# The order of work in a recurrence period, and 704 channels split as 4 x 128 + 2 x 96

## The chip, the cores and the metric

The kernel runs on one core of one Trainium2 chip. The metric is the device time of one execution in microseconds (us). TensorE (PE) multiplies matrices, VectorE (DVE), ScalarE (ACT) and GpSimd (POOL) work on elements, and SyncE (SP) issues transfers between memory and the core's buffers. Everything is computed in float32.

## The reference

Two layers over x of shape 16 x 512 x 256 (16 sequences, 512 time steps, 256 channels), each sublayer followed by a layer norm of its sum with its input:

```
x = layernorm(x + attention(x))             # 16 heads, latents of 32, rotary, causal softmax
x = layernorm(x + fp4_mlp(x))               # 256 -> 704 (gate, up) -> 256
x = layernorm(x + recurrence(x))            # 16 heads, state of 64, 512 steps
x = layernorm(x + channel_mix(x))           # r * (relu(k)^2 @ Wv)

fp4_mlp:      h = silu(q(x) @ q(Wg).T) * (q(x) @ q(Wu).T);  q(h) @ q(Wd).T
              # q: 4-bit grid with one scale for each block of 16 channels, kept as float32
recurrence:   xn = x * rsqrt(mean(x^2) + eps) * norm_w
              state = tanh(state @ tanh(a) + xn_t @ b)           # one after the other in t
              out   = x + (state @ c + skip * xn) @ Wout + bout
channel_mix:  xr, xk = mix of x_t and x_(t-1);  sigmoid(xr @ Wr) * (relu(xk @ Wk)^2 @ Wv)
```

## The kernel before

The kernel has two stages.

**The first stage** goes over the 16 sequences. Its loop is over slots of attention scores (four groups of heads and three slots of rows each). Between the pieces of a slot it takes steps from a list written by hand (PLAN, line 635) that hold the other work: head projections, latents, values, output projection, and the feed-forward tiles of the two sequences before. A feed-forward tile has 128 tokens. `ffn_up` makes its 704 channels, `fp4` quantizes them on DVE and POOL, and `ffn_down` (line 312) turns them into the layout that the down product needs: six transposes on PE into two PSUM banks, evacuated by ACT (lines 323, 325, 326) into the tile hT. Then six matmuls (line 158) accumulate over the channels into ps_d, each with one part of hT as weights and one part of wdT, the down weights, as the moving operand. A float32 matmul of this kind appears in the trace as two instructions. The 704 channels are cut as five parts of 128 and one of 64, so hT and wdT are filled to 128 rows in five parts, and to 64 in the sixth. The three feed-forward tiles of the last sequence that remain are done in the second stage, where DVE evacuates and each product is cut in two halves of 64 output rows.

**The second stage** is the recurrence over 512 time steps, for all 16 sequences at once. The heads form two groups, g = 0 and 1. A step of one group is a recurrence block on PE (`advance_state`, line 1054: 4 matmuls, 8 in the trace) that adds state times ta to what lies in a PSUM bank u, and a tanh on ACT (line 1062) that writes the new state into hist. The inputs of a step, xn times b, are put into u ahead of time (`inputs`, line 1016). While ACT computes the tanh of one group, PE works on the other group and on pieces of other work. PE's order is fixed by the program; the other engines' order is found by a scheduler that simulates the program.

This other work is cut into periods of 16 steps. In period M, `beside(M)` gives the list of its pieces, each a call of a generator up to its next `yield`:

- N, `normed`: the first piece loads 256 tokens (SP), squares and sums them on DVE (line 855), and scales them on POOL (lines 859 to 863); the second transposes them on PE (ps_xn) and DVE writes the result to xt (line 868).
- R, `read_out`: matmuls of the clean states with wc into one bank (line 1032), and the addition of the skip on DVE into ot (line 1039).
- A, `out_of_recurrence`: four products with woutT (ps_a, line 900), then the residual, the statistics and the norm on DVE and POOL (x3, lines 917, 82 to 90, 887).
- M, `mixes`: four transposes of x3 (ps_x), the copy x3T (line 930), the difference d (line 934), and the two mixes muk and mur (line 938), on DVE.
- K, `key`: four products (ps_k); relu on DVE (ka, line 954) and the square on POOL.
- G, `gate`: four products (ps_rr); tanh on ACT (th, line 971).
- V, `value`: four products (ps_kv); on DVE th times ps_kv, the sum x, statistics, norm (o, lines 986 to 992); SP writes o out.

All of these share two PSUM banks of the pool ps_2. A piece that opens a new tile there waits until what was in its bank has been read. A fixed weight is yielded with each piece, and `some` hands out pieces so that a share of the period's total weight is spent in each step: 0.3 of it between the two groups' blocks, 0.7 after both. The pace comes from the table TIME (line 1097). The list of a period before is, from `beside` (line 1069):

```
for name, i in (
    ("N", M + 2), *[("K", old)] * 4, *[("G", old)] * 2, ("R", p), *[("G", old)] * 2,
    *[("A", p)] * 4, *[("V", old)] * 3, ("M", p), ("N", M + 2), ("V", old),
):
```

with p = M - 1 and old = M - 2. History copies (lines 1185 to 1193) on POOL and DVE move the states of eight steps at a time from hist to the clean tiles that the read-out takes.

Of the kernel before, what the change touches and what calls it, by code (L numbers as in the profile page):

```python
# [19 lines left out]
P = 128  # L20
# [3 lines left out]
FF = 704  # L24
NFB = 6
LN_EPS = 1e-5
RMS_EPS = 1e-4
# [30 lines left out]
def tile_kernel(ctx: ExitStack, tc: tile.TileContext, I: dict, out: bass.AP):  # L58
# [156 lines left out]
    def ffn_weights():  # L215
# [20 lines left out]
        for r in range(2):  # L236
            w = ffn.tile([P, FF], F32, tag="h", name="w", bufs=2)
            nc.sync.dma_start(w, I["w_down"][r * P : r * P + P, :])
            wq4 = ffn.tile([P, FF], F32, tag="hq", name="wq4", bufs=2)
            for _ in fp4(wq4, w, FF // 16):  # L240
                pass
            yield 0.3
            for k0 in (0, 3):
                ps = mm("ps_t")
                for kb in range(k0, k0 + 3):
                    n = min(P, FF - kb * P)
                    at = (kb - k0) * P
                    nc.tensor.transpose(ps[:n, at : at + P], wq4[:, kb * P : kb * P + n], ident)
                    nc.scalar.copy(wdT[:n, kb, r * P : r * P + P], ps[:n, at : at + P])
                yield 1.5  # L250
# [61 lines left out]
    def ffn_down(b, j):  # L312
        vector_done(("h", b, j))
        hq, x = hq_of.pop((b, j)), x_of[b][:, j, :]
        hT = ffn.tile([P, NFB, P], F32, tag="hT", name="hT")
        for k0, k1 in ((0, 4), (4, NFB)):
            ps = mm("ps_h")
            for kb in range(k0, k1):
                n = min(P, FF - kb * P)
                at = (kb - k0) * P  # L320
                nc.tensor.transpose(ps[:n, at : at + P], hq[:, kb * P : kb * P + n], ident)
            if k0 == 0:
                copier[0](hT[:, 0:4, :].rearrange("p k t -> p (k t)"), ps)  # L323
            else:
                copier[0](hT[:, 4, :], ps[:, :P])
                copier[0](hT[:64, 5, :], ps[:64, P : 2 * P])
        yield 0.7, True
        ps = mm("ps_d")
        for kb in range(NFB):
            n = min(P, FF - kb * P)  # L330
            product_of[0](ps[:, :C], hT[:n, kb, :], wdT[:n, kb, :], kb == 0, kb == NFB - 1)
            if kb < NFB - 1:
                yield 0.43, False
        nc.vector.tensor_tensor(x, ps[:, :C], x, ALU.add)
        layernorm(x, x)
        at_row = xs.rearrange("(t b) c -> b t c", b=B)
        nc.sync.dma_start(at_row[b, j * P : j * P + P, :], x)
        if j == NT - 1:
            x_of.pop(b)
        yield 0.45, True  # L340
# [507 lines left out]
    def normed(p):  # L848
# [17 lines left out]
        for cc in range(2):  # L866
            for t, at, n in in_ring(cc, p * TS):
# [3 lines left out]
                )  # L871
        yield 0.45

# [28 lines left out]
    def out_of_recurrence(p):  # L902
# [6 lines left out]
        for i in range(2):  # L909
            own = slice(i * C, i * C + C)  # L910
            for cc in range(2):
                product(ps[:, own], ot[:, cc, i * P : i * P + P], sq["woutT"][:, cc, :], cc == 0)
                if cc == 0:
                    yield 0.43
            if i == 0:
                yield 0.43
        nc.vector.scalar_tensor_tensor(
# [5 lines left out]
        normalized(x3, x3, mv)  # L923
        yield 0.43

    def mixes(p):
# [8 lines left out]
        for mu in ("muk", "mur"):  # L935
            mx = mix_of[p, mu] = wk2.tile([P, 2, 2 * P], F32, tag=mu, name=mu)
            for cc in range(2):
                nc.vector.scalar_tensor_tensor(
                    mx[:, cc, :], d[:, cc, :], col(mu, cc), xT[:, cc, : 2 * P], ALU.mult, ALU.add
                )  # L940
        yield 0.45

    def key(p):
        ps, mx = mm("ps_k"), mix_of.pop((p, "muk"))
        ka = ka_of[p] = wk2.tile([P, 2, 2 * P], F32, tag="ka", name="ka")
        for dc in range(2):
            own = slice(dc * 2 * P, dc * 2 * P + 2 * P)
            for cc in range(2):
                product(ps[:, own], sq["wkT"][:, cc, dc * P : dc * P + P], mx[:, cc, :], cc == 0)
                if cc == 0:  # L950
                    yield 0.43
            if dc == 0:
                yield 0.43
        nc.vector.tensor_scalar(ka.rearrange("p c t -> p (c t)"), ps, 0.0, None, ALU.max)
        nc.gpsimd.tensor_tensor(ka, ka, ka, ALU.mult)
        yield 0.43

    def gate(p):
        ps, mx = mm("ps_rr"), mix_of.pop((p, "mur"))
        th = th_of[p] = wk2.tile([P, 2, C], F32, tag="th2", name="th2")  # L960
        for i in range(2):
            own = slice(i * C, i * C + C)
            for cc in range(2):
                product(ps[:, own], mx[:, cc, i * P : i * P + P], sq["wrT"][:, cc, :], cc == 0)
                if cc == 0:
                    yield 0.43
            if i == 0:
                yield 0.43

        for i in range(2):  # L970
            nc.scalar.activation(th[:, i, :], ps[:, i * C : i * C + C], AF.Tanh, scale=0.5)
        yield 0.43

    def value(p):
        ps, ka, th, x3 = mm("ps_kv"), ka_of.pop(p), th_of.pop(p), x3_of.pop(p)
        mv = small.tile([P, 4, 2], F32, tag="mv", name="mv")
        for i in range(2):
            own = slice(i * C, i * C + C)
            for dc in range(2):
                product(ps[:, own], ka[:, dc, i * P : i * P + P], sq["wvT"][:, dc, :], dc == 0)  # L980
                if dc == 0:
                    yield 0.43
            if i == 0:
                yield 0.43
        th, x3 = th.rearrange("p i c -> p (i c)"), x3.rearrange("p i c -> p (i c)")
# [7 lines left out]
        for i in range(2):  # L993
            t0 = p * TS + i * 8
            nc.sync.dma_start(out.rearrange("(b t) c -> t b c", t=T)[t0 : t0 + 8], o[:, i, :])
        yield 0.43

# [25 lines left out]
    def read_out(p):  # L1023
# [3 lines left out]
        for g in range(2):  # L1027
            states = clean.pop((p, g))
            for k in range(2):
                for sel in range(2):  # L1030
# [3 lines left out]
                        states[:, :, k, sel, :], start=True, stop=True, skip_group_check=True,  # L1034
                    )
        for g in range(2):
            for t, at, n in in_ring(g, p * TS):
# [4 lines left out]
                )  # L1042
        yield 1.2

# [24 lines left out]
    def beside(M):  # L1069

        todo = []
        p, old = M - 1, M - 2
        if M == 0:
            todo += [("N", 1)] * 2
        for name, i in (
            ("N", M + 2), *[("K", old)] * 4, *[("G", old)] * 2, ("R", p), *[("G", old)] * 2,
            *[("A", p)] * 4, *[("V", old)] * 3, ("M", p), ("N", M + 2), ("V", old),
        ):
            if 0 <= i < T // TS:
                todo.append((name, i))  # L1080
        return todo + LATER.get(M, [])


# [13 lines left out]
    TIME = {  # L1097
        "E": 0.0, "F": 0.0, "N": 0.22, "K": 0.43, "G": 0.43, "R": 1.2, "A": 0.43, "V": 0.43, "M": 0.45, "U": 0.57, "D": 0.47,
    }
# [16 lines left out]
    with tc.manual_schedule(engines={mybir.EngineType.PE}):  # L1116
# [79 lines left out]
        for e in todo:  # L1196
            step(*e)
        for M in (T // 16, T // 16 + 1, T // 16 + 2):
            for e in beside(M):
# [92 lines left out]
```

## Time and profile before

| what | value |
|---|---|
| median of 3 runs | 2659.92 us (2654.66 to 2662.92) |
| profiled execution | 2657.72 us |
| its span, first to last instruction | 2655.9 us |
| mean granted TensorE clock | 0.975 |
| PE busy | 2480.2 us, 93% of the span |
| DVE, ACT, POOL busy | 73%, 61%, 40% |
| first stage | about 0 to 1790 us |
| recurrence | about 1885 to 2622 us |
| first and last read-out begin | 1906.45 and 2627.72 us |

The profile is of one execution, which is close to the fastest and the median of the runs. In the lines that follow, a row of the timeline gives start, length, engine, line, operation, what is written and read, the array shape of a matmul as rows*columns of weights, the shape of the moving operand, and the number of instructions. Brackets give the idle time before the row and what ended it. A matmul's length contains a modelled tail, so that rows overlap; the distance between two starts is what PE spent. "issue" as the end of an idle time means that the profile shows no other instruction that was waited for.

### The profile page before, as it was taken

How to read it: one execution, taken by the hardware profiler on the slowest of the kernel's cores; microseconds unless marked ns; L12 is line 12 of the kernel's file. 1: busy time of each engine (PE TensorE's matmuls, PEld its weight loads, DVE VectorE, ACT ScalarE, POOL GpSimd, SP SyncE). 2: the span in 40 equal slices, each digit the busy share in tenths (PEclk: the TensorE clock that was granted, in tenths of full speed). 3: DMA queues.
4: the chain of work that ended last, by engine and by line, in shares of the span. 5: the costliest groups of instructions: out<-in, count | busy, mean ns of one | idle time of the engine just before them, and what ended most of it. 6: DMA issues, size and time to landing. Idle time of an engine off the chain costs nothing.

```text
span 2655.9 us, 73932 instructions
## 1 busy us (share of the span) xinstructions
PE 2480.2 (93%) x28802; PEld 1724.5 (65%) x28802; DVE 1926.2 (73%) x5624; ACT 1616.4 (61%) x5593; POOL 1050.6 (40%) x1649
## 2 busy tenths in 40 slices
PE   7788999999999999999999999976899999999997
PEld 4455666666666666666666666554677777777775
DVE  6765888788887888878888888766656655666655
ACT  4655666666666666666666666642366666666663
POOL 4321333333333333333333333322545555555553
PEclk9898999999999999999999999987899999999999
DMA  3000000000000000000000000000101111111100
GB/s 113 23 9 5 11 23 13 15 15 13 24 11 15 15 21 15 13 13 23 13 15 15 11 15 13 7 15 4 47 29 35 39 38 39 39 35 38 35 27 22
DMA packets 58017, 61.31 MB, mean 23 GB/s; under 512 B 7873, under 2 KB 53058, under 8 KB 57666
## 3 DMA queue, kind: packets, MB, share of 16 engines
q1 hardware_dynamic: 56802, 55.54, 6.9%
q8 instruction: 226, 3.70, 0.6%
q14 instruction: 125, 1.02, 0.1%
q10 hardware_dynamic: 864, 1.05, 0.1%
HBM read 39.79 MB, written 16.78 MB: 21 GB/s over the span
## 4 chain that ended last, share of the span: by engine, by line
PE 62%; DVE 24%; ACT 6%; issue 3%; POOL 3%; DMA 1%; SPq 1%; ACTq 0%; POOLq 0%; DVEq 0%
PE ps_pt L562 7%; PE u L1054 7%; PE S L527 6%; PE ps_d L158 5%; PE pg L158 4%; PE pu L158 4%; PE py L593 4%; PE u L1016 4%; DVE p L539 3%; PE ps_h L442 3%; ACT p L552 3%; PE ps_a L900 2%; PE ps_k L900 2%; PE ps_rr L900 2%; PE ps_kv L900 2%
## 5 line engine op out<-in xcount | busy, mean ns | idle before, releaser
L552 ACT ACTIVATE p<-p,nm 128x512 f32<-128x512 f32 (+3 forms) x1024 | 569.5, 561 | 518.3 <-DVE nm L539 513.8
L1062 ACT ACTIVATE hist<-u 64x64 f32<-64x64 f32 x2048 | 444.2, 218 | 282.0 <-PE u L1054 210.5
L539 DVE CUSTOM_DVE_ANT_0 p<-S,mask 128x512 f32<-128x512 f32 (+3 forms) x1024 | 442.5, 483 | 77.8 <-PE S L527 77.7
L562 PEld LDWEIGHTS ps_pt<-ident,p 128*128 128x128 f32 x2560 | 296.0, 142 | 244.8 <-issue 99.6
L1054 PEld LDWEIGHTS u<-hist,ta 128*64 128x64 f32 x8176 | 364.3, 139 | 125.3 <-ACT hist L1062 46.6
L564 ACT COPY pT<-ps_pt 128x384 f32<-128x384 f32 (+1 forms) x768 | 371.7, 515 | 85.5 <-PE ps_pt L562 85.4
L562 PE MATMUL ps_pt<-ident,p 128*128 128x128 f32 x2560 | 398.3, 282 | 7.9 <-DVE nm L539 4.2
L1054 PE MATMUL u<-hist,ta 128*64 128x32 f32 x8176 | 392.9, 219 | 10.3 <-ACT hist L1062 9.8
L212 POOL TENSOR_TENSOR q_q<-q_q,q_m 128x256 f32<-128x256 f32 (+1 forms) x142 | 166.8, 1175 | 488.9 <-DVE q_q L211 483.8
L527 PE MATMUL S<-kc,qr 32*128 32x512 f32 (+3 forms) x2048 | 238.2, 475 | 11.6 <-ACT qr L481 9.5
L1016 PE MATMUL u<-xt,wb 128*64 128x64 f32 x4128 | 224.2, 231 | 2.6 <-issue 2.4
L158 PE MATMUL ps_d<-wdT,hT 128*128 128x256 f32 x732 | 192.9, 408 | 7.3 <-ACT hT L323 6.0
L552 ACT ACTIVATION_READ_ACCUMULATOR p<-p,nm 128x1 f32 x1024 | 198.7, 194 | 0.0
L158 PE MATMUL pg<-wgT,xqT 128*128 128x352 f32 x512 | 177.3, 469 | 7.9 <-ACT xqT L288 4.7
L158 PE MATMUL pu<-wuT,xqT 128*128 128x352 f32 x512 | 174.8, 464 | 0.0
L476 POOL TENSOR_TENSOR qc<-qc,qs 128x512 f32<-128x512 f32 x64 | 81.5, 1274 | 231.2 <-DVE qs L475 216.3
L1016 PEld LDWEIGHTS u<-xt,wb 128*64 128x64 f32 x4128 | 166.0, 139 | 8.4 <-issue 3.0
L158 PEld LDWEIGHTS ps_d<-wdT,hT 128*128 128x128 f32 x732 | 136.5, 200 | 47.8 <-issue 16.2
L593 PEld LDWEIGHTS py<-pT,vpad 128*32 128x32 f32 x5120 | 139.3, 110 | 39.5 <-issue 32.4
L593 PE MATMUL py<-pT,vpad 128*32 128x128 f32 x5120 | 160.6, 275 | 2.7 <-ACT pT L564 2.5
L527 PEld LDWEIGHTS S<-kc,qr 32*128 32x128 f32 x2048 | 110.3, 184 | 79.4 <-issue 40.4
L82 POOL TENSOR_SCALAR ve<-mv 128x2 f32<-128x2 f32 (+1 forms) x160 | 30.7, 192 | 322.1 <-DVE mv L90 318.1
(168 smaller groups left out, 4613.6 us busy)
## 6 DMA issues: line engine op xcount, KB each, us to landing
xT<-in_xT_dram SPq DMA_DIRECT2D x16, 512.0 KB
x<-in_x_dram SPq DMA_DIRECT2D x16, 512.0 KB
xs<-x SPq DMA_DIRECT2D x64, 128.0 KB
x<-xs SPq DMA_DIRECT2D x32, 256.0 KB
xm<-xs SPq DMA_DIRECT2D x32, 256.0 KB
out_dram<-o SPq DMA_DIRECT2D x64, 128.0 KB
w<-in_w_down_dram SPq DMA_DIRECT2D x2, 352.0 KB
w<-in_w_gate_dram SPq DMA_DIRECT2D x5, 128.0 KB
```

The source lines that it names most:

```text
L158: nc.tensor.matmul(dst, left, right, start=start, stop=stop)
L212: nc.gpsimd.tensor_tensor(q, q, m, ALU.subtract)
L527: nc.tensor.matmul(S[h][:, at : at + w], q[rs, i * P : i * P + P], k[rs, :w], start=True, stop=True,)
L539: nc.vector.tensor_tensor_reduce(out=p[:, own], in0=S[h][:, own], in1=mask[:, T - (i + 1) * P :], scale=1.0, scalar=-MASKED, op0=ALU.add, ...
L552: nc.scalar.activation(p[:, own], p[:, own], AF.Exp, bias=nm[:, u : u + 1], scale=-1.0, accum_out=sum_of[b, g][:, cb, half, h : h + 1],)
L562: nc.tensor.transpose(ps[:, at : at + P], p[:, at : at + P], ident)
L564: nc.scalar.copy(pT[:, :w], ps[:, :w])
L593: nc.tensor.matmul(py[q * 32 : q * 32 + 32, PLACE[i][1], :], vpad[b % 2][:, j, g * 4 + h, :], pt, start=j == 0 and h % 2 == 0, stop=j == i ...
L900: nc.tensor.matmul(dst[cs], left[:, cs], right, start=first, stop=not first)
L1016: nc.tensor.matmul(u[rs, k, par:n:2, bs : bs + 16], wb[:, g * 2 + k, par, half, rs], xt[:, g, at : at + n - par : 2, :], start=par == 0 an ...
L1054: nc.tensor.matmul(into[cs, :, c, :], ta[:, t % 2, g * 2 + k, cs], own[:, :, c, :], start=False, stop=True, skip_group_check=True,)
L1062: nc.scalar.activation(state[g][rs, :, r * 32 : r * 32 + 32].rearrange("p k (s b) -> p k s b", s=2), u[rs, :, t - t0, :] .rearrange("p k ( ...
```

## The change

There are two parts.

The 704 channels between the up and down products are cut as four parts of 128 and two of 96. Transposes, weights and down products follow the new table PARTS, and the last two parts, now equally high, are evacuated by one copy of 96 x 256 in place of two copies.

In the second stage the list of a period is written as PERIOD in another order. N's first piece comes after the first K, all four G come together, the read-out R comes after them and is cut in two pieces (one for each group of heads), N's second piece comes directly after A, and M comes in the middle of the four V. The yielded weights and the table TIME get other numbers, and the loop after the last step runs over one more value of M.

```diff
+PARTS = [(0, P), (P, P), (2 * P, P), (3 * P, P), (4 * P, 96), (4 * P + 96, 96)]
...
         for k0, k1 in ((0, 4), (4, NFB)):
             ps = mm("ps_h")
             for kb in range(k0, k1):
-                n = min(P, FF - kb * P)
-                at = (kb - k0) * P
-                nc.tensor.transpose(ps[:n, at : at + P], hq[:, kb * P : kb * P + n], ident)
-            if k0 == 0:
-                copier[0](hT[:, 0:4, :].rearrange("p k t -> p (k t)"), ps)
-            else:
-                copier[0](hT[:, 4, :], ps[:, :P])
-                copier[0](hT[:64, 5, :], ps[:64, P : 2 * P])
+                (of, n), at = PARTS[kb], (kb - k0) * P
+                nc.tensor.transpose(ps[:n, at : at + P], hq[:, of : of + n], ident)
+            w = (k1 - k0) * P
+            copier[0](hT[:n, k0:k1, :].rearrange("p k t -> p (k t)"), ps[:n, :w])
...
         for kb in range(NFB):
-            n = min(P, FF - kb * P)
+            n = PARTS[kb][1]
             product_of[0](ps[:, :C], hT[:n, kb, :], wdT[:n, kb, :], kb == 0, kb == NFB - 1)
...
     def read_out(p):
...
                         states[:, :, k, sel, :], start=True, stop=True, skip_group_check=True,
                     )
+            if g == 0:
+                yield 0.5
         for g in range(2):
...
-        yield 1.2
+        yield 0.5
...
+    PERIOD = [
+        "K-2", "N2", "K-2", "K-2", "K-2", "G-2", "G-2", "G-2", "G-2", "R-1", "R-1", "A-1", "A-1",
+        "A-1", "A-1", "N2", "V-2", "V-2", "M-1", "V-2", "V-2",
+    ]
...
     TIME = {
-        "E": 0.0, "F": 0.0, "N": 0.22, "K": 0.43, "G": 0.43, "R": 1.2, "A": 0.43, "V": 0.43, "M": 0.45, "U": 0.57, "D": 0.47,
+        "E": 0.0, "F": 0.0, "N": 0.3, "K": 0.46, "G": 0.46, "R": 0.5, "A": 0.46, "V": 0.46, "M": 0.6,
+        "U": 0.6, "D": 0.47,
     }
...
-        for M in (T // 16, T // 16 + 1, T // 16 + 2):
+        for M in range(T // 16, T // 16 + 4):
```

The number after a letter in PERIOD is added to M. The down weights (line 248) take the same table PARTS. The weights that the pieces yield change as in TIME: 0.43 to 0.46 for K, G, A and V, 0.45 to 0.6 for N and M.

## Prediction

> **What bounds the kernel now.** I read the page first, its span and chain. TensorE (PE) carries the chain, so both parts of the change are judged by what they do to PE.
>
> ```profile
> span 2655.9 us, 73932 instructions
> ...
> PE 62%; DVE 24%; ACT 6%; issue 3%; POOL 3%; DMA 1%; SPq 1%; ACTq 0%; POOLq 0%; DVEq 0%
> ```
>
> Then the table by stretches, one of the attention and feed-forward stage, one of the recurrence. PE is busy for 98% and 96% at a granted clock of 1.00; no other engine is near it.
>
> ```profile
> 300.00:1750.00 1450.00, 1414.19 (x11230) 930.76 (x11226) 1181.67 (x3537) 943.64 (x2862) 496.00 (x585) 1.00 0.05 15
> 1960.00:2550.00 590.00, 563.64 (x12148) 452.67 (x12145) 361.26 (x991) 373.96 (x1699) 336.20 (x720) 1.00 0.13 36
> ```
>
> Third, PE's timeline of one period of 16 time steps (read-out to read-out). The second column contains a modelled tail, so lengths are taken from start to next start. A recurrence block (L1054 x8) without a wait is 0.20, an input block (L1016) 0.26, a product (L900) 0.46, the read-out (L1032) 1.00, four transposes (L879) 0.59.
>
> ```profile
> 2104.59 0.38 PE L1054 MATMUL u<-hist,ta 128*64 128x32 f32 x8
> 2104.90 1.07 PE L1032 MATMUL ro<-c,wc 128*32 128x256 f32 x16
> ...
> 2106.41 0.38 PE L1054 MATMUL u<-hist,ta 128*64 128x32 f32 x8
> 2106.95 0.42 PE L1054 MATMUL u<-hist,ta 128*64 128x32 f32 x8 [0.15 <-ACT hist L1062]
> ...
> 2117.26 0.42 PE L1054 MATMUL u<-hist,ta 128*64 128x32 f32 x8
> 2118.12 0.66 PE L879 MATMUL ps_xn<-ident,xn 128*128 128x128 f32 x4 [0.43 <-DVE x3T L930]
> ...
> 2121.13 0.43 PE L1016 MATMUL u<-xt,wb 128*64 128x64 f32 x8
> 2121.74 0.65 PE L900 MATMUL ps_k<-muk,wkT 128*64 128x256 f32 x4 [0.18 <-DVE xt L868]
> ...
> 2127.35 0.38 PE L1054 MATMUL u<-hist,ta 128*64 128x32 f32 x8
> 2127.86 1.07 PE L1032 MATMUL ro<-c,wc 128*32 128x256 f32 x16
> ```
>
> The period is 22.94 (27 of them from 1966.37 to 2585.79), but 32x0.205 + 16x0.26 + 16x0.46 + 1.00 + 2x0.585 = 20.25. So 2.7 us a period is no work. It stands at: a step that holds no other work (2106.41 to 2106.95, and again at 2120.35), where PE waits for tanh, 0.33 over its 0.20 plus 0.05 on the block after, so 0.38, twice; the normed transposes, 0.86 for a 0.20 block, of which I put 0.10 down to the change of array shape, so 0.56; the first key product, 0.61 for 0.26, so 0.35; the second read-out, 0.51 against the 0.31 before the first, so 0.20. The rest is two waits of 0.14 for an input bank (2114.82, 2126.72) and changes of array shape.
>
> Fourth, DVE in that period: the transposes wait for the copy that frees their bank, the key product for the normed tile's second half, the read-out for ka.
>
> ```profile
> 2117.37 0.69 DVE L930 COPY x3T<-ps_x 128x512 f32<-128x512 f32 x1 [0.54 <-PE ps_x L879]
> 2121.22 0.47 DVE L868 TENSOR_SCALAR xt<-ps_xn,cols 128x256 f32<-128x256 f32 x1
> 2127.03 0.68 DVE L954 TENSOR_SCALAR ka<-ps_k 128x512 f32<-128x512 f32 x1
> ```
>
> Last, the down product, in narrow windows of the timeline.
>
> ```profile
> 682.98 0.79 PE L158 MATMUL ps_d<-wdT,hT 128*128 128x256 f32 x2
> 683.29 0.70 PE L158 MATMUL ps_d<-wdT,hT 64*128 64x256 f32 x2
> 683.61 0.38 PE L158 MATMUL ps_d<-wdT,hT 64*128 64x256 f32 x1
> 683.92 0.33 PE L562 MATMUL ps_pt<-ident,p 128*128 128x128 f32 x1
> ```
>
> Full-height matmuls start 0.215 apart (681.04, 681.26, 681.47 and on); around the 64-row part it is 0.31, 0.32, 0.31. The weight loads there show why: 0.33 idle before 683.29 and before 683.92, ended by "issue". They are not fetched ahead.
>
> **Part 1, the split of 704.** Count and columns of the matmuls stay: 12 of 256 columns a tile. What goes is the 64-row shape: 0.10 + 0.10 + 0.10 = 0.29 for each of 61 first-stage tiles (64*128 has x122), 17.8 us of PE. That needs 96 rows to run like 128; no row of the trace has 96. The Trainium skill, TensorEngine Tiling (Array Packing), section Tiling Modes, lists 128, 64 and 32 rows only, so 96 must fall to 128; it adds that changing the mode drains TensorE. By TensorE: Matmul & The Clock Gate, Part 2, a drain is about 128 cycles, estimated 53 ns, which for one change in and one out gives 0.11 a tile, 6.5 us; the row says 0.29 and I take the row. Other bound: 96 rows treated as a shape of its own, four such matmuls a tile, 0.10 + 3x0.105 + 0.09 = 0.50 against 0.29: a loss of 0.21x61 = 13 us. How much of it reaches the end lies between PE's 62% of the chain and its 98% busy time in this stage; I take the middle, 80%, 14 of the 17.8.
> The evacuation loses a ScalarE copy: 299 + 276 ns become one of about 375 (the 128x256 copies of L609 and L288), 0.2x61 = 12 us of ACT, which is 65% busy here and 6% of the chain: 0 to 1 us, taken as 0. The last two matmuls now wait for the longer copy, but eight of 0.215 run first. The rewritten weight copies are as many. In the changed order DVE interleaves two quantizations otherwise and POOL does one multiplication earlier, once a sequence; 0, within 2 us either way.
>
> **Part 2, the period.** From the changed kernel's instruction order; t is time after the fourth A product, where PE goes on.
> Removed: one of the two empty steps (0.38). The normed transposes now come right after A and take the read-out's bank, long free (0.56). K takes M's bank, which x3T frees early (0.35). The read-out comes two gate products later, after ka (0.20). Sum 1.49.
> Added: the read-out in two pieces has one more change to the 32-column shape and back. By rows: 0.31 - 0.20 = 0.10 going in, 0.09 of its 1.00 coming out (four groups 0.216 apart, 2104.90 to 2105.57, then 0.31 for the last), 0.05 on the next block: 0.24. Here the same drain rule speaks against the change, at about 0.11; I take 0.24. Net 1.25.
> New positions: (a) M. x3 is normalized 3.08 to 3.81 after A now; one xt eviction (0.45) falls between the two aggregations and delays POOL's rstd, so M can start at 4.1; PE arrives at 4.1 to 4.3. (b) K. On DVE the next tile's two squarings (0.43 each) now stand before x3T, hidden for 0.5 by M's transposes; x3T to 5.9, d to 6.6, first half of muk 7.15; PE arrives after 8.0. (c) Read-out. mur 8.7, th, x, statistics, rstd, o, then ka to 14.75; PE arrives after 15.4. (d) A right after the second piece: ot needs 0.14 + 0.45 after it, PE has 0.66 of steps between. So (a) and (d) are close; 0 to 0.1 each, and I take 0.05 in all: 1.20 a period.
> Queues: SP issues xm ahead of x and the output rows. xm waits for the x3 addition at 0.9, x for POOL's multiplication at about 7; with two buffers each is for the tile after next, 15 us early against the 2.8 of 2113.95 to 2116.72 (issue to POOL's add). On POOL the norm's 0.19 + 0.69 + 0.94 move behind xm's addition and before the second half's history copies, which the read-out needs only at 15. On ACT the two th tanhs move two steps, no more of them. The new yield weights move nothing else; the longer final loop issues nothing.
> 28 full periods x 1.20 = 34, and 1 for each of the last two, which have no N: 36 us.
>
> **Sum.** The profiled execution took 2657.7 (span 2655.9 and 1.8 around it): 2657.7 - 36 - 14 = 2607.7. The median of the runs is 2.2 above that execution, so 2610.
>
> **Rivals.** (1) The period half delivers: A waits for ot or M for x3, 0.6 comes back: 2660 - 18 - 14 = 2628. For: margins near zero. Against: those rows are short. (2) Part 1 does not do what it says, 96 rows keep a shape of their own: 2660 - 36 + 0 to 13 = 2624 to 2637. Against: the page's list; no row decides. (3) More than worked: waits for banks vanish too, 1.7 a period, and all 17.8: 2660 - 50 - 18 = 2592. (4) Slower: DVE's loop becomes the bound. A, x3, M, mix, value's tail, ka, read-out, ot, A is a ring; in before it closes in 14.7 to ka and 8.2 from there to A, which is the period. Now the gate products leave it: 14.75 + 5.6 = 20.4 against PE's 21.7. If the squarings ahead of x3T stalled on their load or the tail came late, each us over 1.3 is paid 28 times; it decides against the change from about 3.1 us (1.3 + 1.2 + 14/28): at 4, 2660 + 25 = 2685. DVE is busy 14.2 of 22.9 and the loads are early, so this is unlikely. (5) Nothing to see, within 0.3% (8 us, about what a measurement can tell from no change).
>
> **Numbers.** Chances: as worked 0.54, (1) 0.16, (2) 0.11, (3) 0.09, (4) 0.07, (5) 0.03. Faster 0.90, same 0.03, slower 0.07. The range runs from (3) at 2592 to the bad end of (2), 2637.
>
> **What would show it.** No 64*128 rows at L160; down products 0.215 apart throughout. Read-outs 21.7 apart; no wait of ps_xn for x3T, of ps_k for xt, of ro for ka; one empty step; two read-out pieces of 0.5. Wrong: 96*128 rows starting 0.31 apart; ps_a waiting for ot or ps_x for x by 0.3 or more; the period still above 22.3.

## The result and the profile after

| | before | after |
|---|---|---|
| median | 2660.86 us (6 runs, 2654.66 to 2663.18) | 2615.54 us (6 runs, 2610.37 to 2617.46) |
| span of the profiled execution | 2655.9 us | 2612.1 us |
| mean granted TensorE clock | 0.975 | 0.979 |
| first recurrence block, first read-out | 1881.62, 1906.45 us | 1864.37, 1890.56 us |
| first to last read-out | 721.27 us | 694.02 us |
| mean period, read-out to read-out | 22.95 us | 22.08 us |

The ratio is 0.983 (95% interval 0.9815 to 0.9846), 45.3 us less, where 2610 was predicted. The forecast and its range held. But the mean period was to fall by 1.20 us and fell by 0.87.

The page of after begins with the span and, lower down, the chain's shares.

```profile
span 2612.1 us, 73864 instructions
...
PE 53%; DVE 30%; ACT 7%; POOL 4%; issue 4%; DMA 1%; SPq 1%; ACTq 0%; POOLq 0%; DVEq 0%
```

PE's share of the chain fell from 62% to 53%, DVE's rose from 24% to 30%. The table by stretches says in which stage PE has been relieved (length, then busy time of PE, PE's weight loads, DVE, ACT, POOL, the granted clock, the DMA share and GB/s):

```profile
300.00:1740.00 1440.00, 1402.12 (x11149) 937.58 (x11146) 1179.75 (x3532) 940.92 (x2810) 495.66 (x585) 1.00 0.05 15
1920.00:2510.00 590.00, 578.50 (x12614) 466.25 (x12612) 396.69 (x1018) 389.51 (x1762) 337.58 (x740) 1.00 0.13 38
```

In the recurrence PE is now busy for 578.50 of 590 us, against 563.64 of 590 before: it does more in the same time. The first stage is as full as before, but has less work to do.

PE's timeline of one period of after, in the same form as that of before:

```profile
2080.24 0.37 PE L1053 MATMUL u<-hist,ta 128*64 128x32 f32 x8
2080.54 0.64 PE L1029 MATMUL ro<-c,wc 128*32 128x256 f32 x8
2081.11 0.42 PE L1053 MATMUL u<-hist,ta 128*64 128x32 f32 x8
...
2081.93 0.64 PE L1029 MATMUL ro<-c,wc 128*32 128x256 f32 x8
2082.50 0.42 PE L1053 MATMUL u<-hist,ta 128*64 128x32 f32 x8
...
2087.15 0.66 PE L876 MATMUL ps_xn<-ident,xn 128*128 128x128 f32 x4
...
2090.78 0.44 PE L876 MATMUL ps_x<-ident,x 128*128 128x128 f32 x2
2091.53 0.44 PE L876 MATMUL ps_x<-ident,x 128*128 128x128 f32 x2 [0.32 <-DVE x L884]
2091.90 0.66 PE L1053 MATMUL u<-hist,ta 128*64 128x32 f32 x16
...
2094.21 0.38 PE L1053 MATMUL u<-hist,ta 128*64 128x32 f32 x8
2094.74 0.42 PE L1053 MATMUL u<-hist,ta 128*64 128x32 f32 x8 [0.15 <-ACT hist L1061]
2094.99 0.43 PE L1013 MATMUL u<-xt,wb 128*64 128x64 f32 x8
2095.25 0.60 PE L897 MATMUL ps_k<-muk,wkT 128*64 128x256 f32 x4
```

Three of the waits shown of before are gone: the normed transposes (2087.15) have none, the first key product starts 0.26 after its input block (2094.99 to 2095.25), and the read-out starts 0.30 after its block, as the first read-out of before did (0.31), where it waited for nothing. One empty step is left (2094.21 to 2094.74). New is a wait in the middle of the mixing transposes: two at 2090.78, the other two only at 2091.53. It is the largest entry in PE's list of waits over 1920 to 2510 us (total, times, longest):

```profile
PE ps_x L876 <- DVE x L884: 7.5, 23, 0.5
PE u L1053 <- ACT hist L1061: 4.0, 26, 0.2
```

The list counts 0.32 us each time. From start to next start the four transposes take 1.12 us (2090.78 to 2091.90) where 0.59 is free of waits, so the step loses 0.53 us in a period that has this wait. What they wait for is the second normalization of x3. DVE's timeline around it, and POOL's:

```profile
2087.99 0.17 DVE L92 BATCH_NORM_AGGREGATE mv<-bnst 128x2 f32<-128x6 f32 x1
2088.07 0.45 DVE L865 TENSOR_SCALAR xt<-ps_xn,cols 128x256 f32<-128x256 f32 x1
2088.44 0.17 DVE L92 BATCH_NORM_AGGREGATE mv<-bnst 128x2 f32<-128x6 f32 x1
...
2089.78 1.70 DVE L884 TENSOR_SCALAR x<-x,mv,rstd 128x256 f32<-128x256 f32 x2 [0.80 <-POOL rstd L86]
```

```profile
2089.05 0.69 POOL L86 TENSOR_TENSOR rstd<-ve,neg_half 128x2 f32<-128x2 f32 x1
2089.92 1.40 POOL L902 TENSOR_TENSOR xm<-xm,bout 128x512 f32<-128x512 f32 x1 [0.18 <-DMA xm<-xs]
```

The two normalizations take 1.70 us together. In the trace of before the same pair took 0.73, and POOL's addition of the output bias began when the pair was nearly done:

```profile
2116.10 0.73 DVE L887 TENSOR_SCALAR x<-x,mv,rstd 128x256 f32<-128x256 f32 x2 [1.17 <-POOL rstd L84]
2116.72 1.27 POOL L905 TENSOR_TENSOR xm<-xm,bout 128x512 f32<-128x512 f32 x1 [0.65 <-DMA xm<-xs]
```

In after the addition begins at 2089.92, behind the start of the first normalization (2089.78) and 0.18 ahead of the second. The second ends at 2091.48, 0.16 us after the addition. This was the first theory for the missing 0.33 us: DVE and POOL keep each other out.

The trace of after holds a comparison of its own. In four periods (normalizations at 2134, 2289, 2355 and 2509) the addition came at least 0.28 us behind the start of the second normalization, as here:

```profile
2134.05 0.74 DVE L884 TENSOR_SCALAR x<-x,mv,rstd 128x256 f32<-128x256 f32 x2 [0.80 <-POOL rstd L86]
2134.66 1.59 POOL L902 TENSOR_TENSOR xm<-xm,bout 128x512 f32<-128x512 f32 x1 [0.65 <-DMA xm<-xs]
```

There the pair keeps its 0.74 us, the transposes do not wait, and the period is 21.60 to 21.69 us. The other full periods have 22.13 or more.

For the first part, PE's groups of the down product, by shape (busy, mean ns):

```profile
L160 PE MATMUL ps_d<-wdT,hT 128*128 128x256 f32 x488 | 126.6, 406 | 7.4 <-ACT hT L323 6.2
L160 PE MATMUL ps_d<-wdT,hT 96*128 96x256 f32 x244 | 63.6, 383 | 0.0
```

There are no 64*128 rows left. The mean length contains the tail, so the starts decide: in the trace the step from 128 to 96 rows, from one part of 96 to the next, and back to 128 are each 0.215 to 0.220 us, and so is the step inside a part of 96. The three steps of 0.31, 0.32 and 0.31 are gone. The twelve matmuls of one tile (eight of 128 rows and four of 96) take 2.60 us up to the next transpose, where those of before took 2.88 (681.04 to 683.92):

```profile
676.27 2.76 PE L160 MATMUL ps_d<-wdT,hT 128*128 128x256 f32 x12
678.87 0.60 PE L559 MATMUL ps_pt<-ident,p 128*128 128x128 f32 x4
```

What this is worth to the stage is read from the first to the last of its 732 down products (starts, in before, after, and in e9, which has 96 rows but keeps both copies):

```profile
L158 PE MATMUL ps_d<-wdT,hT x732: 376/379/796, 235.5 to 1857.0; 128*128 128x256 f32 x183
L160 PE MATMUL ps_d<-wdT,hT x732: 377/379/796, 235.1 to 1842.7; 128*128 128x256 f32 x122, 96*128 96x256 f32 x61
L160 PE MATMUL ps_d<-wdT,hT x732: 377/379/795, 238.0 to 1849.5; 128*128 128x256 f32 x122, 96*128 96x256 f32 x61
```

That is 1621.5, 1607.6 and 1611.5 us. From before to after it is 13.9 us less.

### The profile page after: what moved, and what is told of

Same layout as the page of the kernel before. It is cut to its first block, busy times and chain, and to the rows that moved or that the text cites. A ratio compares the mean times of both kernels' runs of the same rounds, so it can differ in the third digit from the quotient of the medians.

```text
span 2612.1 us, 73864 instructions
## 1 busy us (share of the span) xinstructions
PE 2451.8 (94%) x28802; PEld 1725.3 (66%) x28802; DVE 1946.2 (75%) x5621; ACT 1613.5 (62%) x5532; POOL 1044.0 (40%) x1649
## 4 chain that ended last, share of the span: by engine, by line
PE 53%; DVE 30%; ACT 7%; POOL 4%; issue 4%; DMA 1%; SPq 1%; ACTq 0%; POOLq 0%; DVEq 0%
PE u L1053 7%; PE ps_pt L559 5%; DVE p L536 5%; PE S L524 5%; PE u L1013 4%; PE pg L160 3%; PE pu L160 3%; ACT p L549 3%; PE ps_d L160 3%; PE ps_h L439 3%; PE py L590 2%; PE ps_a L897 2%; PE ps_k L897 2%; PE ps_rr L897 2%; DVE q_q L213 2%
## 5 line engine op out<-in xcount | busy, mean ns | idle before, releaser
L1053 PE MATMUL u<-hist,ta 128*64 128x32 f32 x8176 | 384.5, 219 | 4.8 <-ACT hist L1061 4.6
L524 PE MATMUL S<-kc,qr 32*128 32x128 f32 (+3 forms) x2048 | 238.1, 474 | 11.6 <-ACT qr L478 9.5
L160 PE MATMUL ps_d<-wdT,hT 128*128 128x256 f32 x732 | 180.2, 398 | 7.4 <-ACT hT L323 6.2
L1187 POOL COPY c<-hist 64x256 f32<-64x256 f32 x256 | 111.3, 435 | 65.6 <-ACT hist L1061 56.1
```

Source lines behind the costliest of these rows:

```text
L160: nc.tensor.matmul(dst, left, right, start=start, stop=stop)
L524: nc.tensor.matmul(S[h][:, at : at + w], q[rs, i * P : i * P + P], k[rs, :w], start=True, stop=True,)
L1053: nc.tensor.matmul(into[cs, :, c, :], ta[:, t % 2, g * 2 + k, cs], own[:, :, c, :], start=False, stop=True, skip_group_check=True,)
```

## Experiments

Each kernel was timed beside runs of before, and "below before" is against those. Kernels that were not timed together are compared by their ratios and periods, since the median of before lay at 2661.6, 2657.8 or 2659.8 us.

### The two parts alone

The split of the channels alone, on the kernel before (e1, and once more as e10):

```diff
+PARTS = [(0, P), (P, P), (2 * P, P), (3 * P, P), (4 * P, 96), (4 * P + 96, 96)]
...
+            copier[0](hT[:n, k0:k1, :].rearrange("p k t -> p (k t)"), ps[:n, :w])
```

> The kernel before with the 4 x 128 + 2 x 96 split alone. Theory: the two parts of the change touch different stages (attention and channel mixing until about 1880 us, the recurrence after it), so they add. The first stage ended 14.4 us earlier in the profile of after and the first read-out started 15.9 us earlier, so this alone gives 2643 to 2648 us, 13 to 18 us below before; the recurrence period stays at 22.94 us. Rival: a part of the 16 us at the first read-out came from the new order already acting at the seam between the stages; then this gives only 10 to 12 us, and the first recurrence step is late again.

Measured: 2646.17 us, 15.5 below before, ratio 0.9945 (0.9931 to 0.9959). The mean period stayed at 23.0 us.

The order of the period alone, with its weights and the read-out in two pieces (e2; the channels as before):

> The kernel before with the new order of the recurrence period, its times and the read-out in two pieces alone, the channels split as before. Theory (additive): first to last read-out 694 us instead of 721, so 2630 to 2635 us, 26 to 30 us below before, with a period of 22.1 us. Rival: the two parts overlap at the seam, then the sum of this run's gain and of the split's gain is over 3 us away from the 45.3 us of the whole change.

Measured: 2628.27 us, 33.4 below before, ratio 0.988 (0.9862 to 0.9898), mean period 22.10 us. The time is a little below the 2630 to 2635 expected. The two gains add to 48.9 with e1 and to 45.7 with e10, against 45.3 for the whole. In the first case that is 3.6 away, just past the 3 that were set; but the split alone gave 15.5 and 12.3 when it was timed twice, so the difference is no larger than that spread. The parts add within it.

The traces say where e2's gain lies. From first to last read-out it has 695.2 us, 26.1 less than before. From the last down product of the first stage to the first read-out it has 46.6 where before has 49.4 and e1 49.3, so 2.8 us of the order's gain lie at the seam between the stages, and none of the split's. The first stage itself is as long as before (1621.6 us). The rest of the 33.4 is not explained by the trace; single executions differ by as much before the first down product (235.5 us in before, 241.0 in e8, whose first stage is the same).

The chain moves with the split alone. It has 51% PE and 33% DVE in e1, and 63% and 22% in e2. So with the 64-row matmuls PE held more of the first stage; without them more of the chain runs through DVE, in the softmax (its first line goes from 3% to 5%) and the quantization. That this is why a part of the saved PE time is lost is a reading of the chain; no run tests it.

### The read-out in one piece

```diff
-            if g == 0:
-                yield 0.5
...
-        yield 0.5
+        yield 1.0
...
-        "K-2", "N2", "K-2", "K-2", "K-2", "G-2", "G-2", "G-2", "G-2", "R-1", "R-1", "A-1", "A-1",
+        "K-2", "N2", "K-2", "K-2", "K-2", "G-2", "G-2", "G-2", "G-2", "R-1", "A-1", "A-1",
```

> The kernel after, with the read-out in one piece again (one entry R of weight 1.0 in the period's list instead of two of 0.5); all else as in after. The split costs 0.24 us a period in changes of matmul form (0.31 + 0.25 around the pieces in the profile of after). Theory S: it buys nothing but a more even spread, so undoing it gives back 0.15 to 0.24 us a period, 4 to 6 us: 2609 to 2612 us. Rival S2: with 1.0 us of read-out in one stretch one group's recurrence step waits and one more place stands empty (0.32 us and 0.05): 0.1 to 0.2 us a period slower, 2618 to 2621 us.

Measured: 2618.36 us (2612.32 to 2621.66), ratio 0.984 (0.9821 to 0.9859): by the time not to be told from after. The period tells it: 22.24 in most periods against 22.13. Position by position, the split's shape changes are gone, and behind the read-out one step stands empty (0.53 us, and 0.05 on the block after it). PE's list of waits over 1920 to 2510 us shows the second wait for tanh in each period, 53 where after has 26:

```profile
PE u L1051 <- ACT hist L1059: 8.1, 53, 0.2
```

So rival S2 holds: the split costs 0.29 and pays for itself by filling a step worth 0.38.

### Is it POOL's addition?

In e4 the addition stays, but is queued behind POOL's squaring of ka, a place where POOL was idle for 1.3 us. PE's order of work is that of after.

```diff
-        nc.gpsimd.tensor_tensor(x, x, bout.unsqueeze(1).to_broadcast([P, 2, C]), ALU.add)
+        with tc.issue_after(squared[p - 2].ins) if p >= 2 else nullcontext():
+            nc.gpsimd.tensor_tensor(x, x, bout.unsqueeze(1).to_broadcast([P, 2, C]), ALU.add)
...
-        nc.gpsimd.tensor_tensor(ka, ka, ka, ALU.mult)
+        squared[p] = nc.gpsimd.tensor_tensor(ka, ka, ka, ALU.mult)
```

> The kernel after, with GpSimd's addition of the output bias (xm + bout, 1.40 us, 128x512) queued behind the squaring of ka two periods' work earlier in GpSimd's order, where GpSimd sat idle from 16.3 to 17.7 us of the period; TensorE's order and all sums stay. Theory C (collision): the second normalization of x3 on VectorE took 1.37 us instead of about 0.4 because the addition ran beside it; without it the pair ends by 4.2 us of the period instead of 5.08, the 0.43 us that TensorE waits in front of the mixing transposes goes, the period falls from 22.1 to 21.6 to 21.75 us, and the time to 2603 to 2609 us. Rival D: the normalization is late because an eviction of xt (0.45 us) stands between the two aggregations on VectorE, and the addition only lies beside it; then the pair still ends after 4.7 us, the wait stays at 0.3 us or more and the time within 3 us of 2615.5. Rival E: the addition at its new place stretches the squaring's readers or delays the copies of states in front of the read-out, and the period grows by 0.1 us or more: over 2618 us.

Measured: 2600.65 us (2598.59 to 2604.37), ratio to before 0.9775 (0.9757 to 0.9793), mean period 21.63 us. That is below the 2603 to 2609 expected; the mechanism is the one of theory C. In most periods e4 has 21.61, as the four periods of after in which nothing collided. DVE's and POOL's timelines in e4:

```profile
2173.86 0.74 DVE L884 TENSOR_SCALAR x<-x,mv,rstd 128x256 f32<-128x256 f32 x2 [0.81 <-POOL rstd L86]
```

```profile
2173.13 0.70 POOL L86 TENSOR_TENSOR rstd<-ve,neg_half 128x2 f32<-128x2 f32 x1
...
2185.16 1.04 POOL L953 TENSOR_TENSOR ka<-ka 128x512 f32<-128x512 f32 x1 [1.45 <-DVE ka L952]
2186.16 1.27 POOL L903 TENSOR_TENSOR xm<-xm,bout 128x512 f32<-128x512 f32 x1
2187.60 1.75 POOL L1188 COPY c<-hist 64x256 f32<-64x256 f32 x4 [0.17 <-ACT hist L1062]
```

The pair takes 0.74 instead of 1.70 us, and starts as long after rstd as in after. The two xt evictions still stand around the second aggregation, so it was not they (rival D). The addition at 2186.16 ends before the history copies that wait for tanh (rival E). PE's list of waits over 1920 to 2510 us has one line left:

```profile
PE u L1054 <- ACT hist L1062: 4.2, 27, 0.2
```

The control is the same edit on the kernel before (e8), where the addition met the normalizations in one full period only.

> The kernel before with only GpSimd's addition of the output bias queued behind the squaring of ka, as in the moved version. In the profile of before the second normalization of x3 ended when the addition began (0.43 us mean, not stretched), so theory C gives nothing: within 3 us of before, the mean of the x3 normalization 0.41 to 0.43 us, and the wait for x3T and xt as before. Rival G (the addition is a burden on the loop of VectorE and GpSimd wherever it stands, and moving it is a gain of its own): 8 us or more below before.

Measured: 2657.58 us, ratio 1.0001 (0.9992 to 1.0009). The normalization's mean was 411 ns against 431 in before; the one collision makes this difference. The addition is no burden by itself: moving it pays only where it stood in the way.

### The same collision removed from the other side

In e5 the addition stays where it was in after, and the second piece of N moves behind the first V, so that no eviction of xt delays the normalizations.

```diff
-        "A-1", "A-1", "N2", "V-2", "V-2", "M-1", "V-2", "V-2",
+        "A-1", "A-1", "V-2", "N2", "V-2", "M-1", "V-2", "V-2",
```

> The kernel after with one swap in the period's list: the second piece of N (normed transposes, then the eviction into xt on VectorE) comes behind the first V instead of in front of it; GpSimd's addition stays where it is in after. The evictions of xt then start about 0.7 us later on VectorE and no longer stand between the two aggregations. Theory C (GpSimd's addition blocks the second normalization of x3, because that one starts after it): the aggregations end 0.37 us earlier, so both normalizations start before the addition (3.83 us of the period) and none is stretched; the mean of the x3 normalization falls from 0.82 to 0.41 us, the 0.43 us wait of the mixing transposes goes, the period is 21.6 to 21.75 us and the time 2600 to 2606 us, though the addition was not moved. Rival D (GpSimd's addition is always in the way once it is at its place): the normalization stays at 0.8 us, the period at 22.0 us or more and the time within 4 us of after's 2615.5. Rival F: the normed transposes at a later place make the evictions of xt stand in front of the normalizations instead; a part of 0.2 to 0.4 us of the wait stays, 2607 to 2612 us.

Measured: 2615.29 us (2610.70 to 2616.40), ratio 0.9834 (0.9821 to 0.9848), mean period 21.97 us. Theory C was right on the operation and wrong on the time. DVE and POOL in e5:

```profile
2179.60 0.74 DVE L884 TENSOR_SCALAR x<-x,mv,rstd 128x256 f32<-128x256 f32 x2 [1.17 <-POOL rstd L86]
2180.25 0.87 DVE L865 TENSOR_SCALAR xt<-ps_xn,cols 128x256 f32<-128x256 f32 x2
2181.03 0.78 DVE L852 CUSTOM_DVE_ANT_0 xn<-x 128x256 f32<-128x256 f32 x1
2181.74 0.08 DVE L852 DVE_READ_ACCUMULATOR2_ANT ss<- 128x1 f32 x1
2181.74 0.41 DVE L852 CUSTOM_DVE_ANT_0 xn<-x 128x256 f32<-128x256 f32 x1
```

```profile
2180.26 1.27 POOL L902 TENSOR_TENSOR xm<-xm,bout 128x512 f32<-128x512 f32 x1 [0.70 <-DMA xm<-xs]
```

The normalizations come first and keep their 0.74. But now the evictions of xt stand behind them, and PE's list of waits has a new first line:

```profile
PE ps_x L876 <- DVE xt L865: 12.2, 26, 0.6
```

The mixing transposes need the PSUM bank that the normed transposes hold, and get it when xt has been evicted (2181.12); they start at 2181.26. They take 0.51 us longer to come than without a wait (0.87 against 0.36 behind their input block). So one wait took the place of the other. None of the three expectations had this case: rival F came nearest in its effect, but named another cause.

The rows show more. The evictions, which read PSUM, ran beside the addition at their usual length (0.87 for two). The first squaring, which reads x twice from SBUF, took 0.78 instead of 0.41 and ended 0.28 after the addition; the second, after it, took 0.41.

### What the row form cost

The kernel before with its two copies kept, and parts of 112 and 80 rows (e7), then of 96 and 96 (e9), beside the split with one copy once more (e10). The diff is that of e7 against e1; e9 has e1's PARTS and 96 in the place of 112 and 80.

```diff
-PARTS = [(0, P), (P, P), (2 * P, P), (3 * P, P), (4 * P, 96), (4 * P + 96, 96)]
+PARTS = [(0, P), (P, P), (2 * P, P), (3 * P, P), (4 * P, 112), (4 * P + 112, 80)]
...
+                copier[0](hT[:112, 4, :], ps[:112, :P])
+                copier[0](hT[:80, 5, :], ps[:80, P : 2 * P])
```

> The kernel before with the channels in four parts of 128, one of 112 and one of 80, and with the two separate ScalarE copies of the kernel before kept. It differs from the 4 x 128 + 2 x 96 split in the row numbers and in the copy that was saved. Theory: what was paid for was only the form of 64 rows (three changes of about 0.10 us a tile, 61 tiles), 80 and 112 rows run at the pitch of 128 (0.215 us) and the saved copy was worth nothing: 2644 to 2648 us, as for the split of 96 alone (2646.2). Rival 1: the saved copy on ScalarE carried a part of it: 2650 to 2657 us with the pitch at 0.215 us. Rival 2: row numbers that are no multiple of 32 have a form of their own: pitch over 0.25 us around the 112 and 80 rows, and 2655 to 2665 us.

> The kernel before with the split 4 x 128 + 2 x 96, but with the last two parts evicted by two ScalarE copies of 96 x 128 each, as the kernel before did, instead of one copy of 96 x 256. The run with 112 + 80 rows and two copies left open why it came out 7 us below before in its median where the split of 96 alone had come out 15 us below, although the matmul pitch was the same. Theory P (row forms alone; the copy is worth nothing): within 3 us of the split of 96 repeated beside it. Rival Q (the saved copy carries a part): 4 to 8 us above the split of 96 repeated beside it, and the end of the first stage late by as much in the profile.

> The split 4 x 128 + 2 x 96 alone once more, unchanged, as the partner of the run with two copies on the same chip in the same rounds. Expected again 13 to 18 us below before.

Measured: e7 2651.07 us (14 runs, 2642.27 to 2655.61), 6.7 below before, ratio 0.9969 (0.9959 to 0.9979); e9 2649.89 us, 9.9 below, 0.9963 (0.9951 to 0.9974); e10 2647.45 us, 12.3 below, just short of the 13 to 18 expected, 0.9953 (0.9935 to 0.9972). In the trace of e7 the starts around the parts of 112 and 80 rows are 0.215 to 0.220 us apart, so they have no form of their own (rival 2 falls). The median of e7, though, lies in the window of rival 1, the saved copy. That is why e9 changes the copy alone. By the time it lies 2.4 us above e10, inside the 3 set for theory P, but the two intervals together leave the copy anything from about -3 to 8 us.

The traces settle more. From the first to the last down product of the first stage the three kernels with 64 rows (before, e2, e8) take 1620.2 to 1621.6 us, e7 and e9 with both copies kept 1611.2 and 1611.5, and the eight with one copy (after, e1, e3, e4, e5, e6, e10, e12) 1606.2 to 1609.8. The groups do not overlap. By their means the row numbers are worth 9.8 us and the saved copy 3.6. So rival Q, that the copy carries a part, has the better case, with one traced execution for each kernel.

### A better spread

The last waste seen was the empty step at the period's end. The first try (e6, on e4) only spread the list over more steps:

```diff
-                pace = sum(TIME[n] for n, _ in todo) / 15.5
+                pace = sum(TIME[n] for n, _ in todo) / 16.2
```

> The kernel with the addition moved, and the spread of the period's list over 16.2 steps of the recurrence instead of 15.5. At 15.5 the list is used up before the last step, which therefore stands empty (0.53 instead of 0.20 us, and 0.05 behind it); at 16.2 the last V falls on that place. Theory: 0.35 us a period, 9 us: a period of 21.25 to 21.35 us and 2590 to 2594 us. Rival: the way from the mixing transposes to the first key product shrinks by 0.46 us, and VectorE's muk comes 0.7 us ahead of it now; if the stretched muk operations come later than that, TensorE waits for muk by up to 0.2 us and the time is 2595 to 2600 us.

Measured: 2627.47 us, ratio 0.9881 (0.9867 to 0.9894), 27 us slower than e4, mean period 22.60 us. PE's list of waits:

```profile
PE ps_a L897 <- DVE ot L1039: 12.2, 26, 0.5
PE u L1014 <- ACT hist L1062: 10.1, 26, 0.4
```

Neither theory nor rival foresaw this. At 16.2 every piece moves, not the last one alone. The second read-out piece and the first A came together, with one recurrence block between them:

```profile
2201.65 0.64 PE L1030 MATMUL ro<-c,wc 128*32 128x256 f32 x8
...
2203.11 0.65 PE L897 MATMUL ps_a<-woutT,ot 128*64 128x256 f32 x4 [0.47 <-DVE ot L1039]
```

The second line of the list, 0.39 us a period, is an input block that waits for tanh behind two recurrence blocks in a row (2209.19). No run separates the two.

The second try (e12, on e4) chose weights that leave all pieces up to M in their places and move only the last V (the yields of `mixes`, `value` and `read_out` change as in TIME):

```diff
-        "E": 0.0, "F": 0.0, "N": 0.3, "K": 0.46, "G": 0.46, "R": 0.5, "A": 0.46, "V": 0.46, "M": 0.6,
+        "E": 0.0, "F": 0.0, "N": 0.3, "K": 0.46, "G": 0.46, "R": 0.55, "A": 0.46, "V": 0.5, "M": 0.7,
...
-                pace = sum(TIME[n] for n, _ in todo) / 15.5
+                pace = sum(TIME[n] for n, _ in todo) / 15.8
```

> The kernel with the addition moved, and weights under which the list of the period lasts to its end with the pieces up to M at their old places: the last two V now stand in one step each of the last two steps instead of both in the last but one (a spread over 15.8 instead of 15.5 steps, R 0.55, V 0.50, M 0.7). The spread over 16.2 had pulled the second read-out piece to within 0.25 us of the first A, which then waited 0.5 us for ot; here both keep their distance. Theory: the one empty place (0.33 us and 0.05) goes and nothing else moves: a period of 21.25 to 21.3 us against 21.63, 9 to 10 us below the kernel with the addition moved (2600.7): 2589 to 2593 us. Rival: the first key product comes 0.38 us earlier behind the mixing transposes and waits for muk, or the recurrence waits elsewhere for ScalarE's tanh; then 2595 to 2601 us.

Measured: 2594.92 us (2592.18 to 2600.42), ratio to before 0.9757 (0.9736 to 0.9777), mean period 21.45 us. PE's list of waits over 1920 to 2510 us is empty, and PE is busy for 589.94 of the 590 us:

```profile
1920.00:2510.00 590.00, 589.94 (x12994) 480.42 (x12990) 379.88 (x1045) 401.59 (x1817) 353.43 (x766) 1.00 0.13 38
```

The period fell by 0.18, half of what was expected. In e4 the empty step had cost 0.33 and 0.05 in the block behind it. With one V in each of the last two steps, the two blocks in front of the last V still take 0.60 from start to next start where 0.41 is free of waits, so 0.19 remains; the list does not show it as a wait. This is the fastest of the kernels here, 65 us below before. Its interval overlaps that of e4 (0.9757 to 0.9793), so the gain over e4 rests on the period.

## Why the prediction was right, and where a term was wrong

**Sum.** Predicted -36 for the order and -14 for the split, 2610; measured -45.3. Alone, the order gave -33.4 and the split -15.5 and -12.3. By the stages of the two profiled executions, which differ by 43.8 us, 13.9 come between the first and the last down product, 27.3 between the first and the last read-out, 1.6 at the seam between the two, 0.7 behind the last read-out, and 0.4 ahead of all. So the split gave what was put, and the order about 29.5 of its 36. The loss is in the main the term (a) below.

**Part 1, the row form: right; its worth: right in the sum, wrong in two terms.** 96 rows run like 128: 0.215 us, where 0.31 stood. The Trainium skill's rule that the prediction weighed (TensorE: Matmul & The Clock Gate, Part 2, with TensorEngine Tiling (Array Packing), section Tiling Modes) gave an estimate of 0.11 us a tile; 0.28 went, so taking the row was right. Of the 17.8 us of PE, 80% were to reach the end, a middle value without proof, and the saved copy was to bring nothing. By the traces the rows brought 9.8 of the 17.8, which is 55%, and the copy 3.6. The two errors nearly cancel, so that the 14 came out as put is in part luck. That a part is lost fits the chain, in which DVE takes over from PE.

**Part 2, what goes: right, and a little more.** The four terms, 0.38, 0.56, 0.35 and 0.20, are gone from the timeline one by one, in sum 1.49. Another 0.15 went that the prediction did not list. Most of it, 0.13, stood at the first A product of before and the block behind it, which took 0.53 and 0.26 from start to start (2109.74 to 2110.53) where 0.46 and 0.20 are free of waits.

**Part 2, what comes: 0.24 predicted, 0.29 measured.** The two pieces take 0.57 each, 0.14 more than the single one of 1.00 (0.09 in the sum); 0.10 going in and 0.05 on the next block were right. The estimate of 0.11 by the drain rule would have been much too low here as well.

**Part 2, (a) the margin of M: the term of the period that failed.** The prediction put x3 normalized at 3.81 after A, M ready at 4.1, PE there at 4.1 to 4.3, and 0.05 for (a) and (d) together. In after PE was there at 4.40 (2090.78 less 2086.38), later than predicted, and still waited: x3 was normalized at 5.10 and the step lost 0.53. In e4, without the collision, x3 is ready at 4.15 (the pair ends at 2174.60, and PE goes on behind A at 2170.45), as the prediction's chain of durations gives it, and PE comes at 4.41 without a wait. So the order of the operations and the lengths were right; what failed is the length of one of them, 1.37 us for an operation that was costed at 0.41. That cost came from periods in which the addition began behind the second normalization. The prediction did see that POOL's addition of xm would stand there, under its queues, and asked only what waits behind it on POOL.

The trace of before already held the collision. In one full period the addition began 0.07 us behind the start of the second normalization (POOL at 2023.93), which then took 1.49 us; that period is 23.89 us long, and PE's list of waits had a line for it, which the prediction did not use:

```profile
PE ps_x L879 <- DVE x L887: 0.9, 1, 0.9
```

The books close: 1.49 and 0.15 gone, less 0.29, is 1.35, from 22.95 to the 21.60 of the periods without a collision; less 0.53 it is 0.82, from 22.95 to the 22.13 of most periods. e4 gives back 0.45 of the mean (22.08 to 21.63) without touching PE's order.

**(b), (c) and (d): right.** There is no wait of ps_k for muk, of ro for ka, or of ps_a for ot in after over 1920 to 2510 us. e6 shows how near (d) was: with one block less between the second read-out piece and A, 0.47 is paid each period.

**The rivals.** Rival (1) named the place (M for x3) and 0.6 a period; 0.53 came where the collision was. By time it was 2628 against 2615.5. Rival (2) fell with the pitch of the 96-row parts. Rival (4), DVE's loop as the bound, did not come, though a DVE operation did lengthen.

The prediction's sign of being wrong, ps_x waiting for x by 0.3 or more, did appear: 7.5 us in 23 waits. The gain survived since what went was three times as large.

## What to carry to other kernels

When an order is changed, look at which operations of DVE and POOL will now run at the same time, not only at what waits for what: a duration taken from a trace in which the neighbour came later does not hold beside it. A group whose mean lies above its shortest (431 against 410 ns here) may hold the one case that shows it. A late wait is often only the first of two: before removing its cause, ask which bank or buffer the waiting work needs next (e5). And in a list that is spread by weights, check the place of every piece after a change of pace (e6), and keep the pieces fixed that feed each other.

## What the runs showed of the hardware

**A normalization on DVE and an addition on POOL held each other up.** A normalization of 128x256 (SBUF to SBUF) takes 0.41 us alone. Started 0.18 us after POOL's addition over 128x512, it took 1.37 and ended 0.16 after it; started ahead of it (e5) or away from it (e4, e8), it took its usual length. The limit lies near 0.1 us: in before it was held when the addition began 0.07 us behind its start (2023.93), and kept its 0.41 in every period in which the addition began 0.09 or more behind. The addition is longer too when it begins while a normalization runs: 1.40 us at 2089.92 against 1.27 at 2116.72, though lengths on POOL are rough. The Trainium skill, SBUF — State Buffer, section Who interferes with whom, states this: a VectorE operation that uses both ports or has two SBUF inputs, and a GpSimd operation that reads SBUF, keep each other out for a whole instruction, and the one issued first goes first. The traces here agree on each point that they touch: the order of start decided, to within 0.1 us (after against e5), the squaring with two SBUF inputs was held (0.78 against 0.41), and the evictions from PSUM were not (0.87 for two). That the ports are the cause is the page's statement; the runs show that the stretch goes when the addition goes elsewhere (e4), and also when the normalizations come ahead of it (e5).

**The form of the array costs per change.** Going to 64 rows, between the two instructions of the 64-row part, and back cost about 0.10 us each in before (0.31, 0.32 and 0.31 against 0.215); 96 rows (after) and 112 and 80 rows (e7) cost nothing (0.215 to 0.220). Changing to the 32-column form of the read-out and back cost 0.10 in (0.30 against 0.20), 0.07 a piece (0.57 against the half of 1.00), and 0.05 on the next block (0.25 against 0.20), in after.
